# Graph attention layer on one core: P1 is added into bank 6 in PSUM, the results stay in PSUM for elu, and the side tasks of the second projection get another order

## The chip, the cores and the metric

The kernel runs on one core of one Trainium2 chip. The metric is the device time of one execution in microseconds (us), in float32 throughout. Names used below: TensorE (PE, with weight loads listed as PEld), VectorE (DVE), ScalarE (ACT), GpSimd (POOL) and SyncE (SP), which here only issues DMAs. PSUM is the memory that matmuls write; it is used in eight banks of 128 x 512 floats. A matmul can be told to add to what its bank holds.

## The reference

The input x has 128 graphs of 64 nodes with 512 features. It is normalized, attended twice, passed through a feed-forward block and added to itself:

```
h  = relu(layernorm(x))
a1 = 4 heads of graph attention:  Wh = h @ W_heads[k]; e = leaky_relu(f1 + f2); softmax over adjacent nodes; attn @ Wh
h1 = elu(a1), heads side by side (2048 features)
a2 = one head of the same attention with W_out (2048 x 512)
o  = elu(a2)
y  = relu(o @ w1 + b1) @ w2 + b2 + o
x + layernorm(y) * gamma + beta
```

## The kernel before

The 8192 rows are cut into 64 tiles of 128 rows (two graphs each) and 16 groups of four tiles. One group is 512 rows. For each group `g` the loop at the end of the kernel issues two stretches:

- **First projection.** Four heads, each one call of `project1`, with side tasks between. The attention of layer 1 is applied to the inputs ahead of the weights (`attend1` fills the `z` tiles), so a head is one product of 512 x 512 blocks, and its result goes through `elu`. The side tasks are the second attention of the group before (`stage_e`).
- **Second projection.** `project2(g)`: 28 steps, four heads for each of seven products. Beside them run `attend1(g + 1)`, the feed-forward block of group `g - 1` (`feed_forward`, which has the lists `tr` for transposes, `ff` for its 14 products and `fin` for its four `finish` tasks: second layer norm, addition of x, output), and `stage_a(g + 2)`: first layer norm (`norms`), transposes of the normalized rows (`transposes`), scores (`project_f`, `scores1`), two softmaxes of 128 x 512 (`attn_weights`, one for each pair of tiles) and the transposes of the attention weights (`transpose_weights`, called the turn below, one for each pair; TensorE transposes `s1A` into `s1pt`, L469).

Every 512 x 512 product is done by `unit` (L257) with seven products of 256 x 256 blocks instead of eight, after Strassen and Winograd. P1 to P7 go to three PSUM banks, which are named after the product that opens them: bank 1 takes P1 and P2, bank 5 takes P5 and P3, bank 6 takes P6, P7 and P4. The four results are

```
C11 = P1 + P2          C12 = P1 + P6 + P5 + P3
C22 = P1 + P6 + P7 + P5    C21 = P1 + P6 + P7 + P4
```

Before the change ScalarE copies P1 to SBUF (`s1`, L268), VectorE adds it to P5 (`s15`) and to P6 (`t`, both L270), and the results are bank 5 + `t`, bank 6 + `s15` and bank 6 + `s1`, each added by VectorE (L577 in the first projection, L618 in the second, L719 and L733 in the feed-forward block). In the first projection `elu` (L538) follows: two ScalarE instructions (L541, L542) and one of VectorE (L543), which read the sum in SBUF.

The order of the work on each engine comes from two things. The Python code gives each instruction a place in the program, and `run` (L248) deals a list of side tasks out evenly over the steps of a unit. A scheduler then orders the instructions of each engine by priority and by its own estimate of when they are ready; `high_priority(AHEAD)` moves what follows a product ahead by 150 places. The result is one fixed queue for each engine, in which an instruction that waits holds all behind it. Weights come through a ring of 11 slots (L238), issued by SyncE in the order of their use; loads of x (for `norms`) and of `xr` (for `finish`) go through the same SyncE queue and share four slots.

Pools that matter here: PSUM has six banks for units and `attend1`, and two for transposes and scores. The softmax of layer 1 has one buffer for `e` and one for its result `s1A`, so the second softmax of a group can write its result only after TensorE has transposed the first.

Of the kernel before, what the change touches and what calls it, by code (L numbers as in the profile page):

```python
# [22 lines left out]
def gat_preln_kernel(  # L23
# [28 lines left out]
    nc = tc.nc  # L52
# [188 lines left out]

    late = []

    def flush_late():
        while late:
            late.pop(0)()
# [10 lines left out]
    def unit(name, product, post, order):  # L257


        own = {1: 1, 2: 1, 5: 5, 3: 5, 6: 6, 7: 6, 4: 6}  # L260
        gb, sb = {}, {}

        def after(p):
            if p in (1, 5, 6):
                nm = {1: "s1", 5: "s15", 6: "t"}[p]
                sb[nm] = wk.tile([P, 2, T], FP, tag=nm, name=f"{nm}_{name}")
                if p == 1:
                    nc.scalar.copy(sb[nm], gb[1])  # L268
                else:
                    nc.vector.tensor_tensor(sb[nm], gb[p], sb["s1"], ALU.add)  # L270
                post(nm, sb[nm])
            elif p == 2:
                post("c11", gb[1], None)
            elif p == 7:
                post("c22", gb[6], sb["s15"])
            elif p == 3:
                post("c12", gb[5], sb["t"])
            else:
                post("c21", gb[6], sb["s1"])

        def part(p, i, n):
            def fn():
                if i == 0:
                    subs[p] = product(p)
                    if p == own[p]:
                        gb[p] = bank(f"g{p}_{name}")
                subs[p][i](gb[own[p]], p == own[p] and i == 0)
                if i == n - 1:
                    with tc.high_priority(AHEAD):
                        after(p)  # L290
            return fn

        subs = {}
        n = product(None)
        return [part(p, i, n) for p in order for i in range(n)]
# [161 lines left out]
    def attn_weights(p):  # L457
        A1[p] = softmax(E1.pop(p), None, 2 * H, "s1", p)
# [17 lines left out]

    def stage_a(g):

        if g >= NG:
            return []  # L480
        p, r = 2 * g, 2 * g + 1

        def norms(p):
            norm1(2 * p)
            norm1(2 * p + 1)
            if p >= 2:
                prefetch(2 * p + 2)
                prefetch(2 * p + 3)

        def transposes(p):  # L490
            transpose_h(2 * p)
            transpose_h(2 * p + 1)

        wait = [lambda: None]
        return [
            lambda: norms(p), lambda: norms(r), lambda: transposes(p), lambda: transposes(r),
        ] + wait + [lambda: project_f(g)] + wait * 2 + [
            lambda: (scores1(g), attn_weights(p)), lambda: None, lambda: attn_weights(r),
        ] + wait * 2 + [lambda: transpose_weights(p)] + wait * 2 + [lambda: transpose_weights(r)]


    ZB = {}
# [42 lines left out]
    def flat(ap):  # L545
        return ap.rearrange("p a b -> p (a b)")

    def quadrant(what):
        return int(what[1]) - 1, int(what[2]) - 1
# [7 lines left out]
    def project1(g, h):  # L557


        z = ZB[g]  # L560
        first = (g, h) == (0, 0)
        if h == 0:
            for b in ("11", "12", "S1", "22"):
                tag = "hS" if b == "S1" else "h" + b
                H1[b] = big.tile([P, H, 2, T], FP, tag=tag, name=f"h{b}_{g}")
        sums = {6: 0, 7: 1, 3: 2}
        blk = {1: "11", 2: "12", 4: "22", 5: "S1"}

        def post(what, a, b=None):
            if what[0] != "c":  # L570
                return
            nm = {"c11": "11", "c12": "12", "c21": "S1", "c22": "22"}[what]
            dst = H1[nm][:, h]
            if b is None:
                elu(flat(dst), flat(a), f"{what}_{g}_{h}")
            else:
                nc.vector.tensor_tensor(dst, a, b, ALU.add)  # L577
                elu(flat(dst), flat(dst), f"{what}_{g}_{h}")
            if what == "c21":
                nc.gpsimd.tensor_tensor(dst, dst, H1["22"][:, h], ALU.add)  # L580

        s = unit(
            f"a{g}_{h}", product_t(h, lambda p: ZSUM[h][sums[p]] if p in sums else z[blk[p]][:, h]),
            post, (1, 2, 6, 5, 7, 3, 4) if first else (1, 6, 5, 2, 7, 3, 4),
        )

        def next_sums():
            if h + 1 < H:
                z_sums(g, h + 1)

        return [
            s[0], lambda: (s[1](), flush_late()), lambda: (s[2](), next_sums()), s[3], s[4],
            lambda: (s[5](), late.append(s[6])),
        ]
# [4 lines left out]
    def project2(g):  # L599
        slot = {1: "11", 2: "12", 3: "12", 4: "22", 5: "S1", 6: "11", 7: "S1"}  # L600
        h1 = dict(H1)
        wh = big.tile([P, G, FO], FP, tag="wh2", name=f"wh2_{g}")
        WH2[g] = wh

        def post(what, a, b=None):
            behind = {"s1": ("11", "S1", "11"), "s15": ("S1", "22", "11"), "c11": ("12", "12", "11")}
            if what in behind:
                dst, x0, x1 = (h1[n] for n in behind[what])
                for h in range(H):
                    nc.gpsimd.tensor_tensor(dst[:, h], x0[:, h], x1[:, h], ALU.subtract)  # L610
            if what[0] != "c":
                return
            r, c = quadrant(what)
            dst = wh[:, 2 * r:2 * r + 2, c * Q:(c + 1) * Q]
            if b is None:
                nc.scalar.copy(dst, a)
            else:
                nc.vector.tensor_tensor(dst, a, b, ALU.add)  # L618

        ms = [H + h for h in range(H)]  # L620
        return unit(
            f"b{g}", product_n(ms, lambda p, i: h1[slot[p]][:, i]), post, (1, 5, 6, 2, 7, 3, 4)
        )
# [61 lines left out]
    def feed_forward(g):  # L685
# [22 lines left out]

        bl = {}

        def post1(what, a, b=None):
            if what[0] != "c":
                return
            if not RT:
                RT.extend(big.tile([P, KC, T], FP, tag=f"rt{i}", name=f"rt{i}_{g}") for i in range(2))
            r, c = quadrant(what)
            dst = RT[r][:, 2 * c:2 * c + 2]
            if b is not None:
                nc.vector.tensor_tensor(dst, a, b, ALU.add)  # L719
                a = dst  # L720
            for k in range(2):
                nc.scalar.activation(
                    dst[:, k], a[:, k], AF.Relu, bias=b1s[:, 2 * c + k:2 * c + k + 1]
                )
            if what == "c21":
                bl[2] = blocks(RT, f"r{g}")

        def post2(what, a, b=None):

            r, c = {"t": (0, 1), "s15": (1, 1), "s1": (1, 0)}.get(what) or quadrant(what)  # L730
            dst = o[:, 2 * r:2 * r + 2, c * Q:(c + 1) * Q]
            eng = nc.vector if what[0] == "c" else nc.gpsimd
            eng.tensor_tensor(dst, a, dst, ALU.add)  # L733
# [8 lines left out]
            nc.vector.scalar_tensor_tensor(y, y, rstd, xr, ALU.mult, ALU.add)  # L742
            nc.sync.dma_start(out=of[ts(t, P), :], in_=y)

        f1 = unit(f"c{g}", product_t(M1, lambda p: bl[1][p]), post1, (1, 2, 6, 5, 7, 3, 4))
        f2 = unit(f"d{g}", product_n([M2], lambda p, i: bl[2][p]), post2, (1, 6, 5, 2, 3, 7, 4))
        return (
            [lambda j=j: transpose_out(j) for j in range(G)], f1 + f2,
            [lambda j=j: finish(j) for j in range(G)],
# [60 lines left out]
    for g in range(NG):  # L810
        if g >= 1:
            side = stage_e(g - 1)
        else:
            side = stage_a(1)
            for i, m in ((6, 4), (11, 5), (16, 6), (21, 7)):
                side.insert(i, lambda m=m: more_sums(m))
        done, n = 0, 6 * H
        for i in range(n):
# [6 lines left out]
                done += 1  # L825
        flush_late()
        attn = attend1(g + 1) if g + 1 < NG else []
        if g >= 1:
            tr, ff, fin = feed_forward(g - 1)
        else:  # L830
            tr, ff, fin = [], [lambda: more_sums(M1), lambda: None, lambda: more_sums(M2), load_rows], []
        if g < NG - 1:
            early = [lambda: z_sums(g + 1, 0)]
            at = 8 if g >= 1 else 0
            run(project2(g), mix(attn, tr) + mix(ff[:at] + early + ff[at:], stage_a(g + 2)) + fin)
        else:
            run(project2(g), tr + [lambda: None] * 6 + ff[:2])
            run(ff[2:], [
                lambda: [scores2(g, j) for j in range(G)], lambda: spread2(g), lambda: None,
                lambda: None, lambda: softmax2(g),  # L840
                *[lambda: None] * 7, lambda: transpose_weights2(g), lambda: None,
                *[lambda j=j: attend2(g, j) for j in range(G)], lambda: None,
            ])
    last = fin
    tr, ff, fin = feed_forward(NG - 1)
    run(tr + ff[:6] + last + ff[6:12] + fin[:2] + ff[12:] + fin[2:])
# [29 lines left out]
```

## Time and profile before

| | |
|---|---|
| median of 11 runs | 2389.02 us (2383.66 to 2392.91) |
| profiled execution, its own time | 2390.47 us |
| its span in the trace | 2388.7 us, 32881 instructions |
| granted TensorE clock, mean | 0.994 |
| TensorE busy | 97% |
| VectorE busy | 61% |
| GpSimd busy | 44% |
| ScalarE busy | 33% |
| DMA | mean 154 GB/s |

A profile like this is read from the busiest engine outwards. TensorE is almost never idle, so the first question is where its few idle stretches lie and what ends them; the busy shares of the other engines are means over a whole group, and say little about the stretch in which one of them is full. Busy time of matmuls overlaps (each is listed with some 380 ns, and a new one starts every 216 ns), so the starts are what to read in a list of matmuls, not the durations.

### The profile page before, as it was taken

What the parts mean: (1) busy time and instruction counts of PE and PEld (TensorE: products, weight loads), DVE (VectorE), ACT (ScalarE), POOL (GpSimd) and SP (SyncE); (2) the same over time, 40 slices, a digit from 0 to 9 for tenths busy, and PEclk for the clock granted to TensorE, in tenths of its full rate; (3) what the DMA queues carried; (4) which work ended last, traced back from release to release, by engine and by line L of the source; (5) the groups of instructions that cost most, each with busy time, mean ns of one, the idle gap of its engine ahead of it and who ended that gap; (6) DMA issues with size and microseconds to landing.
All of it is one profiled execution on the core that took longest, in us unless ns stands there. A gap on an engine that the chain in (4) does not pass through costs nothing.

```text
span 2388.7 us, 32881 instructions
## 1 busy us (share of the span) xinstructions
PE 2321.7 (97%) x11805; PEld 1941.2 (81%) x11805; DVE 1454.4 (61%) x2418; ACT 780.2 (33%) x1383; POOL 1062.3 (44%) x933
## 2 busy tenths in 40 slices
PE   6989999999999999999999999999999999999997
PEld 4868888888888888888888888888888888888885
DVE  6736475574855747466574855748466574754637
ACT  2423415233151432415233151432415233141412
POOL 5771443435444263443534444264443534533334
PEclk9989999999999999999999999999999999999999
DMA  8554454454544445454454534545454453534442
GB/s 302 184 178 139 133 167 129 141 172 133 172 133 149 160 133 172 129 164 143 139 174 130 176 128 145 169 133 177 130 161 146 137 176 129 176 122 154 163 149 97
DMA packets 257808, 366.89 MB, mean 154 GB/s; under 512 B 22216, under 2 KB 145128, under 8 KB 257648
## 3 DMA queue, kind: packets, MB, share of 16 engines
q1 hardware_dynamic: 251024, 343.82, 44.5%
q0 software_dynamic: 4512, 16.78, 1.9%
q10 hardware_dynamic: 2112, 4.19, 0.5%
q8 instruction: 95, 1.56, 0.3%
q14 instruction: 65, 0.53, 0.1%
HBM read 337.45 MB, written 27.26 MB: 153 GB/s over the span
## 4 chain that ended last, share of the span: by engine, by line
PE 92%; POOL 3%; DVE 2%; issue 1%; DMA 1%; ACT 0%; DVEq 0%; SPq 0%; POOLq 0%; ACTq 0%
PE g_b L319 33%; PE g_a L304 31%; PE g_c L304 8%; PE g_d L319 8%; PE pz L519 4%; PE pa L668 2%; PE pzS L519 1%; PE pto L695 1%; PE pth L368 1%; PE s1pt L469 1%; PE pf L378 1%; DMA pw<-in_L_gnn_w_dram 1%; PE s1pe L403 1%; POOL pt L218 0%; POOL pt L219 0%
## 5 line engine op out<-in xcount | busy, mean ns | idle before, releaser
L319 PE MATMUL g_b<-w,h 128*128 128x256 f32 x2560 | 601.4, 381 | 0.0
L319 PEld LDWEIGHTS g_b<-w,h 128*128 128x128 f32 x2560 | 477.8, 190 | 74.6 <-issue 14.0
L304 PE MATMUL g_a<-zs_z,w 128*128 128x256 f32 x1504 | 352.4, 382 | 18.6 <-issue 16.0
L304 PE MATMUL g_a<-z,w 128*128 128x256 f32 x1520 | 359.5, 379 | 1.0 <-ACT at L471 0.9
L304 PEld LDWEIGHTS g_a<-zs_z,w 128*128 128x128 f32 x1504 | 286.7, 192 | 70.0 <-issue 28.3
L304 PEld LDWEIGHTS g_a<-z,w 128*128 128x128 f32 x1520 | 287.7, 190 | 54.5 <-issue 14.6
L319 PE MATMUL g_b<-w,hS 128*128 128x256 f32 x1024 | 248.0, 389 | 6.4 <-DVE z L531 6.4
L580 POOL TENSOR_TENSOR hS<-hS,h 128x512 f32<-128x512 f32 x64 | 81.6, 1276 | 371.5 <-DVE hS L543 368.3
L319 PEld LDWEIGHTS g_b<-w,hS 128*128 128x128 f32 x1024 | 190.5, 192 | 50.4 <-issue 15.7
L610 POOL TENSOR_TENSOR h<-h,h 128x512 f32<-128x512 f32 x64 | 86.8, 1356 | 227.2 <-PE g_b L319 227.2
L542 ACT ACTIVATE exc<-exc 128x512 f32<-128x512 f32 x256 | 160.6, 627 | 6.0
L543 DVE SCALAR_TENSOR_TENSOR h<-exc,h 128x512 f32<-128x512 f32 x128 | 103.7, 810 | 63.4 <-ACT exc L542 63.3
L541 ACT ACTIVATE exc<-h 128x512 f32<-128x512 f32 x128 | 80.5, 629 | 181.5 <-DVE h L577 181.5
L610 POOL TENSOR_TENSOR h<-hS,h 128x512 f32<-128x512 f32 x64 | 81.6, 1275 | 125.1 <-PE g_b L319 125.0
L330 POOL TENSOR_TENSOR zs_z<-z,zs_z 128x512 f32<-128x512 f32 x63 | 87.3, 1386 | 84.9 <-PE g_d L319 73.7
L329 POOL TENSOR_TENSOR zs_z<-zS,z 128x512 f32<-128x512 f32 x63 | 87.7, 1393 | 81.7 <-PE g_a L304 60.7
L331 POOL TENSOR_TENSOR zs_z<-z,zs_z 128x512 f32<-128x512 f32 x63 | 88.9, 1411 | 78.5 <-PE g_a L304 78.5
L319 PE MATMUL g_d<-w,rt 128*128 128x256 f32 x512 | 121.2, 379 | 1.8 <-DVE o L733 1.0
L304 PE MATMUL g_c<-ot,w 128*128 128x256 f32 x512 | 121.1, 379 | 0.7 <-ACT s_c L268 0.7
L304 PE MATMUL g_a<-zS,w 128*128 128x256 f32 x496 | 117.2, 379 | 0.0
L634 DVE SCALAR_TENSOR_TENSOR jf<-wh,ao 128x512 f32<-128x512 f32 x128 | 111.9, 894 | 0.7
L519 PE MATMUL pz<-at,hn 64*128 64x256 f32 x768 | 108.1, 405 | 3.5 <-DVE z L531 3.5
(163 smaller groups left out, 3660.5 us busy)
## 6 DMA issues: line engine op xcount, KB each, us to landing
w<-tc SPq DMA_DIRECT2D x632, 256.0 KB, 2.7
w<-in_L_gnn_W_heads_dram SPq DMA_DIRECT2D x192, 256.0 KB, 2.9
w<-in_L_gnn_W_out_dram SPq DMA_DIRECT2D x192, 256.0 KB, 2.7
w<-in_L_gnn_w_dram SPq DMA_DIRECT2D x96, 256.0 KB, 2.7
x<-in_x_dram SPq DMA_DIRECT2D x66, 256.0 KB, 2.7
xr<-in_x_dram SPq DMA_DIRECT2D x64, 256.0 KB, 2.8
out_dram<-o SPq DMA_DIRECT2D x64, 256.0 KB, 2.2
tc<-pt POOLq DMA_DIRECT2D x20, 512.0 KB, 4.3
```

The source lines that it names most:

```text
L304: nc.tensor.matmul(bk[:, o, :], w[:, k, ts(o, P)], a[:, k, :], start=start and o == 0 and k == 0, stop=k == 1, skip_group_check=True,)
L319: nc.tensor.matmul(bk[:, j, :], a[:, k, ts(j, P)], w[:, k, :], start=start and k == 0 and j == 0, stop=i == len(ms) - 1 and k == 1, skip_g ...
L329: eng.tensor_tensor(s2, s1, a11, ALU.subtract)
L330: eng.tensor_tensor(s4, a12, s2, ALU.subtract)
L331: eng.tensor_tensor(s3, a22, s2, ALU.subtract)
L519: nc.tensor.matmul(banks[b][:, c, :].rearrange("p (h n) -> p h n", h=H), src[rows, off + c * P:off + (c + 1) * P], at[rows, b], start=True ...
L541: nc.scalar.activation(ex, src, AF.Relu, scale=-1.0)
L542: nc.scalar.activation(ex, ex, AF.Exp, scale=-1.0)
L543: nc.vector.scalar_tensor_tensor(dst, ex, -1.0, src, ALU.add, ALU.max)
L580: nc.gpsimd.tensor_tensor(dst, dst, H1["22"][:, h], ALU.add)
L610: nc.gpsimd.tensor_tensor(dst[:, h], x0[:, h], x1[:, h], ALU.subtract)
L634: nc.vector.scalar_tensor_tensor(junk, WH2[g][:, j], 1.0, ao[:, c, :], ALU.mult, ALU.mult, accum_out=f[:, c, j:j + 1],)
```

## The change

In `unit`, ScalarE still copies P1. VectorE then adds P1 to bank 6 in place, in PSUM, after P6, and ScalarE copies that sum (`t`) and P5 (`s5`) to SBUF. P7 and P4 are accumulated on top, so bank 6 ends as C21 without an addition. C12 is added into bank 5 and C22 into bank 1, and `elu` reads all four results from PSUM. In the second product of the feed-forward block, the addition of `s1` to one quadrant of `o` goes.

The order of the products changes: the first projection and the first feed-forward product go to 1, 5, 6, 2, 3, 7, 4 from 1, 6, 5, 2, 7, 3, 4 and from 1, 2, 6, 5, 7, 3, 4; the second feed-forward product goes to the same from 1, 6, 5, 2, 3, 7, 4. The second projection keeps 1, 5, 6, 2, 7, 3, 4.

`stage_a` returns three lists (norms; transposes and scores; turns), and the side tasks of the second projection are dealt out anew: norms go beside `attend1`; two of the four `finish` tasks go between the last feed-forward products, beside the scores; and the other two `finish` tasks go last, beside the two turns. In group 0, the sums of the feed-forward weights (`more_sums(M1)`, `more_sums(M2)`) go from the beginning of that list to its end, and those of the other weights come a few tasks earlier in the first projection.

```
     def after(p):
         if p in (1, 5, 6):
-            nm = {1: "s1", 5: "s15", 6: "t"}[p]
+            nm = {1: "s1", 5: "s5", 6: "t"}[p]
             sb[nm] = wk.tile([P, 2, T], FP, tag=nm, name=f"{nm}_{name}")
-            if p == 1:
-                nc.scalar.copy(sb[nm], gb[1])
-            else:
-                nc.vector.tensor_tensor(sb[nm], gb[p], sb["s1"], ALU.add)
+            if p == 6:
+                nc.vector.tensor_tensor(gb[6], gb[6], sb["s1"], ALU.add)
+            nc.scalar.copy(sb[nm], gb[p])
             post(nm, sb[nm])
         elif p == 2:
-            post("c11", gb[1], None)
+            post("c11", gb[1])
         elif p == 7:
-            post("c22", gb[6], sb["s15"])
+            post("c22", gb[6], sb["s5"], gb[1])
         elif p == 3:
-            post("c12", gb[5], sb["t"])
+            post("c12", gb[5], sb["t"], gb[5])
         else:
-            post("c21", gb[6], sb["s1"])
+            post("c21", gb[6])
...
 # project1
-            if b is None:
-                elu(flat(dst), flat(a), f"{what}_{g}_{h}")
-            else:
-                nc.vector.tensor_tensor(dst, a, b, ALU.add)
-                elu(flat(dst), flat(dst), f"{what}_{g}_{h}")
+            if b is not None:
+                nc.vector.tensor_tensor(to, a, b, ALU.add)
+                a = to
+            elu(flat(dst), flat(a), f"{what}_{g}_{h}")
...
-            post, (1, 2, 6, 5, 7, 3, 4) if first else (1, 6, 5, 2, 7, 3, 4),
+            post, (1, 2, 6, 5, 7, 3, 4) if first else (1, 5, 6, 2, 3, 7, 4),
...
 # stage_a
+        return (
+            [lambda: norms(p), lambda: norms(r)],
+            [
+                lambda: transposes(p), lambda: transposes(r), nothing, lambda: project_f(g), nothing,
+                lambda: (scores1(g), attn_weights(p)), nothing, lambda: attn_weights(r),
+            ],
+            [nothing, lambda: transpose_weights(p), nothing, nothing, lambda: transpose_weights(r)],
+        )
...
 # side tasks of project2, groups 1 to 14 (before: one line)
-            run(project2(g), mix(attn, tr) + mix(ff[:at] + early + ff[at:], stage_a(g + 2)) + fin)
+        first = mix(attn, tr)
+        first[9:9] = norms[:1]
+        first += norms[1:]
...
+            run(project2(g), first + mix(
+                ff[:7] + early + ff[7:12] + fin[:1] + ff[12:13] + fin[1:2] + ff[13:], scores
+            ) + mix(fin[2:], [nothing] + turns + [nothing] * 2))
...
 # feed_forward
-        f1 = unit(f"c{g}", product_t(M1, lambda p: bl[1][p]), post1, (1, 2, 6, 5, 7, 3, 4))
-        f2 = unit(f"d{g}", product_n([M2], lambda p, i: bl[2][p]), post2, (1, 6, 5, 2, 3, 7, 4))
+        f1 = unit(f"c{g}", product_t(M1, lambda p: bl[1][p]), post1, (1, 5, 6, 2, 3, 7, 4))
+        f2 = unit(f"d{g}", product_n([M2], lambda p, i: bl[2][p]), post2, (1, 5, 6, 2, 3, 7, 4))
```

More of the change, by code (lines that the diff above doesn't have):

```diff
@@ L242, in gat_preln_kernel, with nothing @@
     late = []
+    def nothing():
+        pass
     def flush_late():
@@ L479, in stage_a @@
         if g >= NG:
-            return []
+            return [], [], []
         p, r = 2 * g, 2 * g + 1
@@ L492, in transposes @@
             transpose_h(2 * p + 1)
[L494 to L499, printed above, removed]
+        return (
[6 more added lines that the diff above has]
+        )
     ZB = {}
@@ L567, in project1, with post @@
         blk = {1: "11", 2: "12", 4: "22", 5: "S1"}
-        def post(what, a, b=None):
+        def post(what, a, b=None, to=None):
             if what[0] != "c":
@@ L603, in project2, with post @@
         WH2[g] = wh
-        def post(what, a, b=None):
-            behind = {"s1": ("11", "S1", "11"), "s15": ("S1", "22", "11"), "c11": ("12", "12", "11")}
+        def post(what, a, b=None, to=None):
+            behind = {"s1": ("11", "S1", "11"), "s5": ("S1", "22", "11"), "c11": ("12", "12", "11")}
             if what in behind:
@@ L709, in feed_forward, with post1 @@
         bl = {}
-        def post1(what, a, b=None):
+        def post1(what, a, b=None, to=None):
             if what[0] != "c":
@@ L726, in post1, with post2 @@
                 bl[2] = blocks(RT, f"r{g}")
-        def post2(what, a, b=None):
-            r, c = {"t": (0, 1), "s15": (1, 1), "s1": (1, 0)}.get(what) or quadrant(what)
+        def post2(what, a, b=None, to=None):
+            if what == "s1":
+                return
+            r, c = {"t": (0, 1), "s5": (1, 1)}.get(what) or quadrant(what)
             dst = o[:, 2 * r:2 * r + 2, c * Q:(c + 1) * Q]
@@ L813, in gat_preln_kernel @@
         else:
-            side = stage_a(1)
-            for i, m in ((6, 4), (11, 5), (16, 6), (21, 7)):
+            side = sum(stage_a(1), [])
+            for i, m in ((5, 4), (9, 5), (12, 6), (17, 7)):
                 side.insert(i, lambda m=m: more_sums(m))
@@ L827, in gat_preln_kernel, with sums_late @@
         attn = attend1(g + 1) if g + 1 < NG else []
-        if g >= 1:
-            tr, ff, fin = feed_forward(g - 1)
-        else:
[L831 to L834, printed above, removed]
-            run(project2(g), mix(attn, tr) + mix(ff[:at] + early + ff[at:], stage_a(g + 2)) + fin)
[L836 to L843, printed above, removed]
+        norms, scores, turns = stage_a(g + 2)
+        tr, ff, fin = feed_forward(g - 1) if g >= 1 else ([], [], [])
+        if g == NG - 1:
+            run(project2(g), tr + [nothing] * 6 + ff[:2])
+            run(ff[2:], [
+                lambda: [scores2(g, j) for j in range(G)], lambda: spread2(g), nothing, nothing,
+                lambda: softmax2(g), *[nothing] * 7, lambda: transpose_weights2(g), nothing,
+                *[lambda j=j: attend2(g, j) for j in range(G)], nothing,
+            ])
+            continue
+        early = [lambda: z_sums(g + 1, 0)]
+        first = mix(attn, tr)
+        first[9:9] = norms[:1]
+        first += norms[1:]
+        if g == 0:
+            def sums_late(m):
+                fetch(m)
+                weight_sums(m, LAST["A"])
+            run(project2(g), first + early + scores + turns + [
+                load_rows, lambda: sums_late(M1), lambda: sums_late(M2)
+            ])
+        else:
+            run(project2(g), first + mix(
+                ff[:7] + early + ff[7:12] + fin[:1] + ff[12:13] + fin[1:2] + ff[13:], scores
+            ) + mix(fin[2:], [nothing] + turns + [nothing] * 2))
     last = fin
```

## Prediction, as put on record before the changed kernel ran

> **What bounds the kernel now.** I read the busy shares and the chain first, then the waits of TensorE, then each wait in the order of time on the engine named.
>
> ```profile
> PE 2321.7 (97%) x11805; PEld 1941.2 (81%) x11805; DVE 1454.4 (61%) x2418; ACT 780.2 (33%) x1383; POOL 1062.3 (44%) x933
> PE 92%; POOL 3%; DVE 2%; issue 1%; DMA 1%; ACT 0%; DVEq 0%; SPq 0%; POOLq 0%; ACTq 0%
> ```
>
> TensorE is the bound, and the change leaves it every matmul. So it can win only TensorE's idle time, and lose by adding to it. The waits of TensorE (us in total, times, longest):
>
> ```profile
> PE g_a L304 <- issue: 16.0, 13, 2.2
> PE g_b L319 <- DVE z L531: 6.4, 1, 6.4
> PE pz L519 <- DVE z L531: 3.5, 1, 3.5
> ```
>
> The windows by stage (length, PE busy, PEld, DVE, ACT, POOL, granted clock, DMA share, GB/s) say where the idle time lies:
>
> ```profile
> 0.00:60.00 60.00, 39.74 (x182) 27.80 (x183) 40.78 (x112) 16.98 (x29) 34.78 (x51) 1.00 0.84 302
> 60.00:199.00 139.00, 125.67 (x694) 103.49 (x693) 77.16 (x119) 44.55 (x78) 91.09 (x89) 0.95 0.51 175
> 199.00:2216.00 2017.00, 2001.04 (x10225) 1680.12 (x10224) 1238.27 (x2019) 671.55 (x1191) 873.91 (x744) 1.00 0.46 149
> 2216.00:2389.00 173.00, 155.22 (x709) 129.80 (x708) 98.22 (x171) 47.09 (x85) 62.50 (x50) 0.98 0.41 135
> ```
>
> Idle: 20.3 us in the prologue, 13.3 in group 0, 16.0 in the 2017 us of the steady part, 17.8 in the last group. The 16.0 are the 13 waits put down to "issue", one at each start of a first projection after a feed-forward block (2.1, 1.2, 2.1, 0.9, 2.2, then 0.8 to 1.5). The timeline of VectorE and TensorE at such a place shows what they are:
>
> ```profile
> 1217.79 0.69 DVE L270 TENSOR_TENSOR t_a<-g_a,s_a 128x512 f32<-128x512 f32 x1
> 1218.58 3.69 PE L304 MATMUL g_a<-zs_z,w 128*128 128x256 f32 x16 [0.80 <-issue]
> ```
>
> P7 of head 0 may write bank 6 only after VectorE has read `t` from it, and VectorE is late: it still works on the `finish` tasks. In group 0 it is a DMA and GpSimd that make VectorE late:
>
> ```profile
> 138.46 0.69 DVE L340 BATCH_NORM_STATS2 n1st<-x 128x6 f32<-128x512 f32 x1 [9.72 <-DMA x<-in_x_dram]
> 146.27 0.18 DVE L342 BATCH_NORM_AGGREGATE n1mv<-n1st 128x2 f32<-128x6 f32 x1 [6.53 <-POOL n1nb L354]
> ```
>
> Copies of `z` stand behind both, and TensorE waits for their PSUM banks (6.4 and 3.5 us). Last, the place that the new task order touches, the turns (s1pt) of one group, with the scores that feed them:
>
> ```profile
> 1178.48 1.09 PE L403 MATMUL s1pe<-R,L 64*64 64x256 f32 x16
> 1193.42 1.04 PE L469 MATMUL s1pt<-ident,s1A 128*128 128x128 f32 x8
> 1206.38 1.04 PE L469 MATMUL s1pt<-ident,s1A 128*128 128x128 f32 x8
> ```
>
> ```profile
> 1195.22 0.23 DVE L436 COPY s1A<-s1A 128x128 f32<-128x128 f32 x1
> 1202.61 1.67 DVE L742 SCALAR_TENSOR_TENSOR o<-o,n2rs,xr 128x512 f32<-128x512 f32 x1
> ```
>
> The second softmax ends on VectorE at 1195.45, 10.9 us before its turn at 1206.38: no wait.
>
> [...] the trace has 683 to 691 with one input from PSUM (L270). [...] L742 has a median of 753 ns, a mean of 1192, and up to 1860, with the long one above beside a GpSimd sum. [...]
>
> **The change, part by part.** One product of four matmuls takes 1.73 us on TensorE (starts in the timeline), a turn of two tiles 0.87, the scores 1.0.
>
> *Copies and sums.* There are 112 units (64 + 16 + 16 + 16). The P5 addition goes in all of them, the C21 addition in 96: 208 VectorE instructions of 0.685 us, 142 us. `elu` from PSUM (L543: 682 ns) in place of SBUF (810 and 946) saves 128 x 0.128 + 64 x 0.264 = 33 us. ScalarE gets 224 copies of 0.58 = 130 us. Neither engine is the bound, so this is worth only what TensorE waits for them. An addition that writes PSUM is not in the trace; between 0.6 and 0.8 us, I take 0.69.
>
> *New waits inside a unit.* P7 now needs the addition and then a ScalarE copy, 0.69 + 0.58 and three hand-overs of some 0.15 = 1.7 us. P2 and P3 stand between, 3.46 us. Covered with 1.7 us to spare; in the queues of the changed program I find at most one or two instructions (a softmax exponential, an `elu` of the transposed attention) ahead of the copy. With no cover it would cost 1.7 us x 64. P4 after P7 in the last head of each group has half a product (0.86 us) over C22's addition, which takes 0.2 + 0.69 + 0.1: 0.2 us x 15 = 3 us lost (0 to 5). In the last feed-forward block P4 follows P7 directly (about 1 us lost), and P2 no longer follows P1 (0.7 won): nothing in sum.
>
> *The boundary.* Two `finish` tasks earlier, and two products rather than one between P6 and P7: the 16 us go (13 to 16).
>
> *Group 0.* The feed-forward sums leave this stretch except one fetch, so GpSimd does not stand at a DMA there: 9.9 us (6.4 + 3.5), of which I take 10 (6 to 10). The fetches of W_out keep their places nearly. That the other 2.6 and 0.9 stay is assumed.
>
> *The turns.* In the compiled queue of TensorE the turns of groups 1 to 13 now stand together near the end: after the scores come 10 products, the first turn, one product, the second turn. So the second is due 11 x 1.73 + 0.87 = 19.9 us after the scores (before: 1179.50 to 1206.38, 26.9). In the compiled queue of VectorE, the same in all 13 groups, 42 instructions stand from the first masked addition of the scores (L417) to the last copy of the second softmax (L436): both softmaxes, three additions to `o`, four of each instruction of `finish`, two of L618, one of L634. The last `finish` instruction (L742) stands right before that copy. With the mean of each group, the softmaxes are 2 x (0.681 + 0.864 + 0.686 + 0.781 + 0.686 + 0.202 + 0.843 + 0.256) = 10.0 us. The rest: L733 3 x 0.686, L340 4 x 0.682, L342 4 x 0.163, L344 4 x 0.144, L741 4 x 0.798, L742 4 x 1.192, L618 2 x 0.68, L634 0.97: 16.3. Starts follow each other some 0.06 us closer than these durations: 26.3 - 42 x 0.06 = 23.8. ScalarE's exponential leaves VectorE idle for 0.7 in the first softmax, GpSimd some 0.2 before an L742, the start 0.15: 24.8 us. Three of eight transposes can go before the copy; the other five take 0.54. The turn then ends at 24.8 + 0.1 + 0.54 = 25.4, not at 19.9 + 0.87 = 20.8: TensorE stands 4.7 us in each group. (P4 of the second feed-forward product waits for part of that earlier, behind the same queue; it isn't counted twice.) Behind it everything of the group is late by the same time. Bounds: with no instruction stretched by GpSimd (0.68 to 0.75 in place of the means) the copy ends at 22.0 and the wait is 1.9; with all stretched at 26.5, and 6.3. Loss: 13 x 4.7 = 61 us (25 to 82).
>
> *Sum* against the profiled execution's own 2390.5: + 61 + 3 - 16 - 10 = + 38, 2428.5. The median is 1.5 below that execution: 2427.
>
> **Rivals.** *VectorE keeps up (faster).* Were the 42 instructions done within 20.2 us, the turn would not wait, and 2389 - 26 + 3 = 2366 would be left. For it: VectorE loses 175 of 1454 us. Against it: of these 42, none is removed, and the same kinds took 25 us of busy time between 1180.7 and 1210.8. *It cancels (no change).* With the shortest durations the loss of 25 meets the gain of 26: 2391. *ScalarE becomes late inside the heads.* If the copy of `t` stood behind a late exponential by 2 us in each of 64 heads, 0.3 us each, 20 us more: 2447. Against it: the instructions ahead end earlier by the counting above.
>
> **Numbers.** Likeliest, the late turn: 2427, chance 0.80 with its own range; beyond it, by the second mechanism together with the upper bounds, 0.05; keeping up 0.10; cancelling 0.05. Changes within 0.2%, 4.8 us, are about what can't be told from none. Low end: 13 x 2.6 us lost against 26 won, 2396; high end: 82 + 5 against 22, 2454. Faster 0.10, same 0.05, slower 0.85.
>
> **What would show it.** Right: waits of TensorE at s1pt for VectorE's s1A, some 13 of them, 2 to 6 us each, and none at the start of the first projection; group 0 without the waits for `z`; VectorE busy near 1280 us, ScalarE near 910. Wrong: no waits at s1pt, or idle time at g_a inside the heads, in front of P7, for `t`.

## The result, and the profile after

The changed kernel takes 2411.61 us (median of 8 runs, 2409.27 to 2413.58). The kernel before, measured again beside it, takes 2389.26 us (31 runs). The ratio is 1.0095, with a 95% interval of 1.0086 to 1.0103: slower by about 1%. The profiled execution took 2413.58 us with a span of 2411.8 us, 23.1 us more than the span before. I forecast a loss of 38 us; the sign and the place were right, and most of the sizes were off.

The busy shares of the changed kernel say that TensorE is still the bound, that VectorE lost 249 us of work, and that ScalarE gained 132:

```profile
PE 2340.3 (97%) x11805; PEld 1951.5 (81%) x11805; DVE 1205.2 (50%) x2210; ACT 912.1 (38%) x1623; POOL 1027.7 (43%) x917
```

The waits of TensorE in the changed kernel (us in total, times, longest) say where the time went. The 13 waits at g_a are gone, and there are waits at s1pt for s1A. One of the 14 in the first line, 5.4 us, lies in the prologue, in the kernel before too; the other 13 lie in groups 1 to 13. One wait at a copy of `z` remains in group 0.

```profile
PE s1pt L472 <- DVE s1A L435: 32.5, 14, 5.4
PE pzS L525 <- DVE z L537: 5.7, 1, 5.7
...
PE s1pt L472 <- DVE s1A L439: 1.5, 8, 0.2
```

The timeline of TensorE in one group of the changed kernel (start, duration, engine, line) shows the late turn. From 1063.53 eight matmuls of g_b take 1.73 us, so the second turn was due at 1065.26. It starts at 1067.69, 2.43 us late. Then something appears that I hadn't counted: the sixteen matmuls from 1069.52 take until 1073.65, 4.13 us in place of 16 x 0.216 = 3.46, and no wait is marked.

```profile
1062.66 1.04 PE L472 MATMUL s1pt<-ident,s1A 128*128 128x128 f32 x8
1063.53 1.89 PE L322 MATMUL g_b<-w,h 128*128 128x256 f32 x8
1067.69 2.03 PE L472 MATMUL s1pt<-ident,s1A 128*128 128x128 f32 x8 [2.27 <-DVE s1A L435]
1069.52 4.30 PE L322 MATMUL g_b<-w,h 128*128 128x256 f32 x16
1073.65 1.89 PE L307 MATMUL g_a<-z,w 128*128 128x256 f32 x8
```

The windows of the same stretch (length, then busy time of PE, PEld, DVE, ACT, POOL, then the granted clock, third from the end) show what that is: after the pause the granted clock of TensorE is 0.50 for three microseconds.

```profile
1060.00:1064.00 4.00, 4.00 (x25) 3.56 (x24) 3.05 (x9) 1.16 (x3) 1.96 (x2) 1.00 0.86 259
1064.00:1067.50 3.50, 1.42 (x7) 0.92 (x5) 2.65 (x7) 0.37 (x1) 1.74 (x3) 1.00 0.48 170
1067.50:1070.50 3.00, 2.81 (x11) 2.43 (x12) 3.00 (x10) 1.17 (x2) 0.00 (x0) 0.50 0.68 207
```

VectorE in the same group shows why the copy is late. It ends at 1068.34, 23.05 us after the next product began behind the scores (1045.29); 19.97 us was the time to beat. In that stretch VectorE is full, but for 0.70 us in the first softmax, for ScalarE's exponential, which I had counted, and one wait of 1.80 us for GpSimd's n2rs:

```profile
1062.36 0.69 DVE L623 TENSOR_TENSOR wh<-g_b,t_b 128x512 f32<-128x512 f32 x1
1064.85 0.75 DVE L749 SCALAR_TENSOR_TENSOR o<-o,n2rs,xr 128x512 f32<-128x512 f32 x1 [1.80 <-POOL n2rs L349]
...
1066.86 0.69 DVE L435 TENSOR_TENSOR s1A<-s1e,s1r 128x512 f32<-128x512 f32 x1
...
1068.12 0.22 DVE L439 COPY s1A<-s1A 128x128 f32<-128x128 f32 x1
```

GpSimd's own timeline shows that n2rs stood behind the addition to the next `xr`. SyncE issued that load only at 1058.40, behind the output of an earlier finish task, and the two loads of this stretch took 4.2 to 4.5 us to land, so it came at about 1062.9. The profile names VectorE's last instruction as the releaser here, since the two fall together; of the additions to `xr` that wait, 28 wait for the load.

```profile
1063.05 1.27 POOL L745 TENSOR_TENSOR xr<-xr,bs 128x512 f32<-128x512 f32 x1 [2.04 <-DVE wh L623]
1064.27 0.55 POOL L349 TENSOR_TENSOR n2rs<-n2ve,mhalf 128x1 f32<-128x1 f32 x1
```

By stages, the first projection of group 1 begins 6.8 us earlier than before (192.7 for 199.5), the stretch from there to the last first projection is 33.4 us longer (2044.9 for 2011.5), and the rest is 3.5 us shorter (174.2 for 177.7). The sum is the 23.1 us.

### The profile page after: what moved, and what is told of

It reads as the page before. It is cut to its first block, busy times and chain, and to the rows that moved or that the text cites. A ratio compares the mean times of both kernels' runs of the same rounds, so it can differ in the third digit from the quotient of the medians.

```text
span 2411.8 us, 32882 instructions
## 1 busy us (share of the span) xinstructions
PE 2340.3 (97%) x11805; PEld 1951.5 (81%) x11805; DVE 1205.2 (50%) x2210; ACT 912.1 (38%) x1623; POOL 1027.7 (43%) x917
## 4 chain that ended last, share of the span: by engine, by line
PE 82%; DVE 10%; issue 2%; POOL 2%; DMA 2%; ACT 1%; SPq 0%; DVEq 0%; POOLq 0%
PE g_a L307 31%; PE g_b L322 26%; PE g_c L307 8%; PE g_d L322 5%; PE pz L525 4%; PE pa L673 2%; DVE o L749 2%; DVE o L748 2%; PE pzS L525 1%; DMA xr<-in_x_dram 1%; PE pto L700 1%; PE pth L371 1%; DVE n2st L343 1%; DVE o L740 1%; PE s1pt L472 1%
## 5 line engine op out<-in xcount | busy, mean ns | idle before, releaser
L322 PE MATMUL g_b<-w,h 128*128 128x256 f32 x2560 | 614.7, 387 | 0.0
L322 PEld LDWEIGHTS g_b<-w,h 128*128 128x128 f32 x2560 | 488.1, 194 | 78.1 <-issue 13.0
L547 ACT ACTIVATE exc<-g_a 128x512 f32<-128x512 f32 x256 | 152.3, 595 | 199.4 <-DVE g_a L581 119.1
L549 DVE SCALAR_TENSOR_TENSOR h<-exc,g_a 128x512 f32<-128x512 f32 x192 | 131.6, 685 | 137.7 <-ACT exc L548 136.6
L333 POOL TENSOR_TENSOR zs_z<-z,zs_z 128x512 f32<-128x512 f32 x63 | 88.2, 1401 | 117.0 <-PE g_d L322 74.2
L745 POOL TENSOR_TENSOR xr<-xr,bs 128x512 f32<-128x512 f32 x64 | 84.7, 1324 | 77.5 <-DMA xr<-in_x_dram 68.9
L322 PEld LDWEIGHTS g_d<-w,rt 128*128 128x128 f32 x512 | 96.0, 190 | 17.3 <-DVE o L740 1.4
L428 ACT ACTIVATE s1e<-s1e 128x512 f32<-128x512 f32 x32 | 20.2, 630 | 232.1 <-DVE s1e L427 232.1
```

The costliest lines, as they stand in the source:

```text
L322: nc.tensor.matmul(bk[:, j, :], a[:, k, ts(j, P)], w[:, k, :], start=start and k == 0 and j == 0, stop=i == len(ms) - 1 and k == 1, skip_g ...
L333: eng.tensor_tensor(s4, a12, s2, ALU.subtract)
L547: nc.scalar.activation(ex, src, AF.Relu, scale=-1.0)
L549: nc.vector.scalar_tensor_tensor(dst, ex, -1.0, src, ALU.add, ALU.max)
L745: nc.gpsimd.tensor_tensor(xr, xr, bs, ALU.add)
```

## Experiments

My theory at this point: the second turn is late because of its place behind VectorE's queue. The rivals: the new unit costs the time, or the late `xr` does, or the low clock is an effect of its own. Ratios below are against the kernel before, measured on the same chip in the same series, with 95% intervals. "Period" is the time from one group to the next, read from the starts of the matmul s2pe; with no pause at all it turned out to be 142.26 us.

**The two halves apart.** The first kernel is the changed one with the side tasks, the turns and the sums of group 0 as before; the second is the kernel before with the new side tasks.

```
 # unit_only, against the changed kernel (cut short; stage_a and the sums of group 0 go back too)
-            run(project2(g), first + mix(ff[:7] + early + ... , scores) + mix(fin[2:], ...))
+            run(project2(g), mix(attn, tr) + mix(ff[:at] + early + ff[at:], stage_a(g + 2)) + fin)
 # order_only, against the kernel before: the same lines, exchanged
```

> The change of the unit alone (P1 added in PSUM, the new copies, the new orders of products), with the side tasks of the second projection and the sums of group 0 dealt out as in the kernel before. Late turn (my theory): 19 VectorE instructions stand between the scores and the second turn, and the turn is due some 27 us after the scores, so no wait at the turns; the 13 waits at the start of the first projection shrink (P7 comes one product later, the copy costs 0.9 us more), from 16 to 5 us or less; group 0 keeps its waits for copies of z. About 2378 us, 2370 to 2386, faster than the kernel before. Rival, the unit costs it (longer chains, more of ScalarE, other order of products): 2400 us or more.

> The order of the side tasks alone (and the moved sums of group 0), with the unit and the orders of products of the kernel before. Late turn: the same 42 VectorE instructions stand between the scores and the second turn, due 19.9 us after the scores, and more of them are slowed beside GpSimd than in the changed kernel, since VectorE has the additions from SBUF: a wait of 3.4 to 5 us in each of 13 groups, +44 to +65, less some 7 in group 0 and up to 16 at the start of the first projection: 2410 to 2432 us. Rival, the unit costs it: the order of the tasks gains, 2366 to 2385 us.

Measured: the unit alone 2379.74 us, ratio 0.9984 (0.9978 to 0.9991); the order alone 2411.84 us, ratio 1.0111 (1.0096 to 1.0126). The two add up to the whole, -0.16% and +1.11%. The unit is no cost, and the order is all of it. Two things were unexpected. The unit alone keeps the waits at the first projection, only at another product: P4 of the first head now waits for VectorE's addition of C22, which reads the bank that P4 adds to.

```profile
PE g_a L307 <- DVE g_a L578: 13.5, 12, 1.3
PE g_b L322 <- DVE z L534: 10.7, 1, 10.7
```

And the order alone shows the low clock at its plainest, on TensorE: a pause of 1.54 and 0.19 us, and then sixteen matmuls in 5.06 us (1066.83 to 1071.89) that need 3.46.

```profile
1065.44 0.52 PE L472 MATMUL s1pt<-ident,s1A 128*128 128x128 f32 x3 [1.54 <-DVE s1A L435]
1066.15 0.89 PE L472 MATMUL s1pt<-ident,s1A 128*128 128x128 f32 x5 [0.19 <-DVE s1A L439]
1066.83 5.22 PE L322 MATMUL g_b<-w,h 128*128 128x256 f32 x16
```

**The turns early.**

```
-                ff[:7] + early + ff[7:12] + fin[:1] + ff[12:13] + fin[1:2] + ff[13:], scores
-            ) + mix(fin[2:], [nothing] + turns + [nothing] * 2))
+                ff[:7] + early + ff[7:12] + fin[:1] + ff[12:13] + fin[1:2] + ff[13:], scores + turns
+            ) + fin[2:])
```

> The changed kernel with the two turns dealt out with the scores beside the products of the feed-forward block, and the last two finish tasks after them: 22 VectorE instructions in place of 42 before the second turn, which is due some 30 us after the scores. Late turn: the 13 waits of 3.4 us go, 2411.6 - 44 = 2367 us (2363 to 2376), faster than both kernels. Rival, the unit costs it: the same as the changed kernel, 2405 to 2415. Rival, the two finish tasks now last delay the t of the first head: waits at the start of the first projection of 1 to 2 us come back, 2380 to 2393.

Measured: 2354.8 us, ratio 0.9877 (0.9863 to 0.9890), below the range of the expectation: 57 us under the changed kernel where 44 was expected (52 by the two ratios, since the kernel before took 2383.79 us in this series and 2389.26 beside the changed kernel). Each group loses 4.5 us less, not 3.4, since the low clock goes with the pause. Some 0.4 us a group goes that no wait accounts for. The starts of TensorE's matmuls have it where one shape of matmul follows another: the small products of `attend1` (pz) stand in six stretches of each group here, and in seven in the changed kernel. In the steady part TensorE does not stop at all, as the window shows (busy time is the whole length):

```profile
199.00:2180.00 1981.00, 1981.00 (x10172) 1669.44 (x10171) 1031.75 (x1826) 780.94 (x1395) 843.28 (x734) 1.00 0.46 152
```

**The same queue, one product later.** VectorE's 42 instructions stay as they are.

```
-            ) + mix(fin[2:], [nothing] + turns + [nothing] * 2))
+            ) + mix(fin[2:], [nothing] * 2 + turns + [nothing]))
```

> The changed kernel with both lists as they are, but the second turn one product of TensorE (1.73 us) later; the queue of VectorE keeps its 42 instructions between the scores and the last copy. In the changed kernel TensorE stands some 2.4 us for the first copy of s1A and 0.4 for the last, and its granted clock is then at 0.50 for some 3 us, another 1.2 to 1.7 us lost: 4.5 us in a group. Queue against due time, with the clock: the pause falls to 0.6 to 1.1 us, too short for the clock to fall, 1.0 to 1.6 us lost in a group: 2411.6 - 13 x 3.2 = 2370 us (2366 to 2376). Pause alone, the clock costs nothing: only the 1.73 us of each group are saved, 2389 us (2386 to 2394).

Measured: 2373.48 us, ratio 0.9950 (0.9936 to 0.9963). One product of 1.73 us saves 3.0 us a group (period 143.8 for 146.8), and the low clock is gone. This fits the clock theory (2366 to 2376) and not the pause alone (2386 to 2394). TensorE's timeline has the short pauses, and 0.216 us a matmul behind them (1055.88 to 1057.60 for eight):

```profile
1054.57 0.52 PE L472 MATMUL s1pt<-ident,s1A 128*128 128x128 f32 x3 [0.58 <-DVE s1A L435]
1055.27 0.77 PE L472 MATMUL s1pt<-ident,s1A 128*128 128x128 f32 x5 [0.19 <-DVE s1A L439]
1055.88 1.89 PE L322 MATMUL g_b<-w,h 128*128 128x256 f32 x8
1057.60 1.89 PE L307 MATMUL g_a<-z,w 128*128 128x256 f32 x8
```

**The late xr.**

```
 # finish(j)
-            xr = load(t, "xr")
+            if j == 0:
+                for k in range(G):
+                    XR[t + k] = load(t + k, "xr")
+            xr = XR.pop(t)
 # norms(p): two of the four loads of x, for the next group, go behind the finish tasks
```

> The changed kernel with the four loads of xr in a group issued together at the first finish task, and two loads of x moved behind the finish tasks to make room; places of turns and finish tasks kept, and the second turn still due 11 products after the scores. It takes away the 1.8 us that VectorE stands in the 42 instructions for GpSimd's n2rs, which stands behind an addition to a late xr; 38 instructions then stand before the copy. If the queue and that wait make the turn late: the wait of 3.4 us per group falls to 0 to 1.6, 2367 to 2390 us. If the wait for GpSimd is not part of it (VectorE would have been late anyhow): 2405 to 2412.

Measured: 2371.26 us, ratio 0.9947 (0.9933 to 0.9960), period 143.5. In twelve groups the turn is late by 0.6 us only, and the clock stays up. In the last, VectorE has 40 instructions rather than 38 before the copy and waits for GpSimd again, and the turn is 2.8 us late. The wait for GpSimd, 1.8 us in a queue that was 2.6 us too late, may thus have decided whether the late turn was dear; but the queue is shorter by four instructions too, and this run does not separate the two.

Both repairs in one:

> Both repairs in one: turns early, and the four loads of xr together at the first finish task (its loads of x moved behind the finish tasks). If the late xr cost time only through the late turn, there is nothing left for it to win, since TensorE has no pause left in groups 1 to 13: 2352 to 2357 us, the same as with the turns early alone. If late xr costs something of its own: 2340 to 2350. If the x loads, now later, delay the norms: 2360 or more.

Measured: 2365.85 us, ratio 0.9916 (0.9902 to 0.9929). This is 11 us worse than the turns early alone. The later loads of x make VectorE wait inside the norms (2.62 us in one group), C22's addition stands behind that, and in three groups TensorE stands 1.5 us at P4 of the first head for it. The rest is 0.44 us in each group (period 142.7 for 142.26), with no wait in the list: the list is dealt out differently, pz stands in seven stretches again, and the 0.44 us lie in the starts where the shape of matmul changes, 41 times in a group for 39. A load moved out of the way of one queue came late in another.

**All four finish tasks last.** This asks what removed the waits at the first projection.

```
-                ff[:7] + early + ff[7:12] + fin[:1] + ff[12:13] + fin[1:2] + ff[13:], scores + turns
-            ) + fin[2:])
+                ff[:7] + early + ff[7:], scores + turns
+            ) + fin)
```

> The kernel with the turns early, but all four finish tasks behind the feed-forward products, as in the kernel before. If the 13 waits at the start of the first projection came from VectorE's four finish tasks, they are back, now at P4 of the first head (1.1 to 1.4 us each, as with the unit alone): 2354.8 + 13 x 1.3 = 2372 us (2368 to 2378). Rival, the new unit and its order of products removed them: 2353 to 2358 us.

Measured: 2409.86 us, ratio 1.0104 (1.0084 to 1.0124). The waits are back, so the earlier place of two finish tasks is needed to remove them. They are far dearer than I expected: 34.7 us in 13 waits at P7, and the low clock behind them. VectorE shows why. The statistics of the next x stand 5.78 us for their load, which SyncE issues at 1071.79, behind the outputs of the late finish tasks (1069.14), and the addition of P1 stands next in the queue; ScalarE's copy of it and TensorE's P7 follow at once:

```profile
1077.31 0.69 DVE L343 BATCH_NORM_STATS2 n1st<-x 128x6 f32<-128x512 f32 x1 [5.78 <-DMA x<-in_x_dram]
1077.92 0.68 DVE L272 TENSOR_TENSOR g_a<-g_a,s_a 128x512 f32<-128x512 f32 x1
...
1079.33 3.78 PE L307 MATMUL g_a<-zs_z,w 128*128 128x256 f32 x8 [3.46 <-ACT t_a L273]
```

**Group 0.** Three runs, all on the kernel with the turns early. First the sums at their old places:

```
-            for i, m in ((5, 4), (9, 5), (12, 6), (17, 7)):
+            for i, m in ((6, 4), (11, 5), (16, 6), (21, 7)):
...
-            run(project2(g), first + early + scores + turns + [load_rows, lambda: sums_late(M1), lambda: sums_late(M2)])
+            run(project2(g), first + mix(early + [lambda: more_sums(M1), nothing, lambda: more_sums(M2), load_rows], scores + turns))
```

> The kernel with the turns dealt out early (2354.8 us), but the weight sums of group 0 at their places of the kernel before. Sums in group 0: TensorE's waits for copies of z return (6.4 and 3.5 us in the kernel before, 5.7 with the sums moved), 5 to 9 us lost, all of it before the first projection of group 1: 2360 to 2364 us. Rival, the 7 us won ahead of group 1 came from the task order or the unit and not from the sums: 2353 to 2357 us.

Measured: 2354.54 us, ratio 0.9871 (0.9857 to 0.9885), the same as with the sums moved. In place of one wait of 5.7 us at pzS there are two, 3.3 at pzS and 2.4 at g_a. In this kernel, then, moving the sums wins nothing. Next, loads of x on ScalarE's queue:

```
-        nc.sync.dma_start(out=tl, in_=xf[ts(t, P), :])
+        queue = nc.scalar if name == "x" and 2 * G <= t < 3 * G else nc.sync
+        queue.dma_start(out=tl, in_=xf[ts(t, P), :])
```

> The kernel with the turns early (2354.8 us), but the four loads of x for group 2 are issued by ScalarE's queue and not by SyncE's. In every kernel so far SyncE issues the first of them only at 130.5 us, behind eight loads of transformed weights, and copies of z on VectorE stand behind its statistics. If that queue is the cause of TensorE's 5.7 us at pzS in group 0: the wait goes, with the low clock after it up to 8 us won, 2346 to 2351 us. Rival, as my prediction put it, GpSimd's sums make VectorE late there: 2353 to 2357 us, the same.

Measured: 2355.89 us, ratio 0.9893 (0.9879 to 0.9908), nothing won: these were the wrong loads, and SyncE still issued the one in question, at 132.2 us. The scheduler takes norms up a group ahead. The loads of the next group are the right ones (`3 * G <= t < 4 * G`):

> As the run before with loads of x on ScalarE's queue, but now those of group 3: the compiled queue of VectorE shows that the statistics that stand among the copies of z in group 0 are those of tile 12, taken up a group ahead. Its slot is free when the first layer norm of tile 8 ends (124.8 us), SyncE issues its load at 130.7, 5.9 us later, behind loads of transformed weights. If SyncE's queue is the cause of the 5.7 us at pzS: the load lands some 6 us earlier, the wait falls to 0 to 1, with the low clock after it 5 to 8 us won against 2354.8: 2347 to 2350 us. Rival, GpSimd or the transfer is late: 2353 to 2357 us.

Measured: 2348.76 us, ratio 0.9850 (0.9836 to 0.9863). Two timelines show it. With the turns early, SyncE issues the load at 130.66 and VectorE waits 12.06 us; here ScalarE's queue issues it at 124.77, and VectorE waits 5.35. (In the kernel before, SyncE issued the load behind the 9.72 us of the prediction at 130.89, after five loads of transformed weights.)

```profile
130.66 0.41 SPq L95 DMA_DIRECT2D x<-in_x_dram  x1
136.30 0.69 DVE L343 BATCH_NORM_STATS2 n1st<-x 128x6 f32<-128x512 f32 x1 [12.06 <-DMA x<-in_x_dram]
```

```profile
124.77 0.35 ACTq L96 DMA_DIRECT2D x<-in_x_dram  x1
129.53 0.69 DVE L344 BATCH_NORM_STATS2 n1st<-x 128x6 f32<-128x512 f32 x1 [5.35 <-DMA x<-in_x_dram]
```

TensorE's 5.7 us at pzS shrink to one wait of 2.0, and all that follows is 6 us earlier. This version is the fastest of all, 1.5% below the kernel before.

## Why the prediction was right or wrong

- **The late turn: right in mechanism, mis-sized by errors that partly cancel.** Turn due 19.9 us after the scores: measured 19.97. Queue of 42 instructions: the same. "24.8 us" to the end of the copy was too long: 23.05 in the group shown. In the mean of the 13 groups the 42 instructions take 23.4 us and not 26.3. The largest part of that is 1.8 us: I had taken L742 at its mean of 1192 ns, and the same instruction, now L749, has a mean of 766 in the changed kernel (in the kernel before 33 of the 64 stood beside a GpSimd instruction of over 0.9 us for more than half of their time, with a mean of 1610 ns, and 25 met none, 745; in the changed kernel 15, 834, and 48, 746). Another 1.0 is the softmaxes, which I had taken at means too. Against that I had allowed 0.9 us for VectorE's waits, and 2.3 came, 1.8 of them before an L749 in the group shown, where I had 0.2. So the pause was mis-sized: 4.7 predicted, 2.6 measured (gaps between starts, less the matmuls in them: 2.25 before the first transpose and 0.38 before the fourth, the mean of the 13 groups). The term that was missing is the low clock, 1.5 us on average in 12 of the 13 groups (what is left of the gaps, 18 us). Together 52 us for the predicted 61. "The second turn is late" is shown by the run with one product more, which keeps the queue and changes the due time.
- **The boundary: right that the waits go, wrong in the second of its reasons.** I gave two finish tasks earlier, "and two products rather than one between P6 and P7". The unit alone has the new order and keeps 13.5 us of waits; most of them only move from P7 to P4. All four finish tasks last brings them back. So the place of the finish tasks did it. The way differs, though. In the kernel before, VectorE has no wait for a load in the 9 us ahead of any of the 13 waits: there it is its queue alone, as I wrote. In the unit alone it stands 2.6 to 3.6 us for a late x ahead of each of the 12, and with all four last 3.8 to 6.1 ahead of the twelve longest. The gain was more than 16 as well: behind two of the three longest waits of the kernel before, the clock was low too, 1.7 us each, some 19 in all.
- **Middle part.** 52 less 19 is 33, and 33.4 were measured.
- **"P4 after P7 in the last head", 3 us: none.** No such wait is listed, and the group without pauses has none of it. (The sum was off as well: 0.99 less 0.86 is 0.13 us, 2 us in 15 groups.)
- **Group 0: 10 predicted, 6.8 measured, and the cause was wrong.** The sums at their old places cost nothing, in the kernel with the turns early. The wait that stayed, 5.7 us, comes in the main from a load of x that stood in SyncE's queue behind transformed weights, which the last run shows; a wait of 2.0 us is left without it. How the new order of tasks won its part of 6.8 us stays open: by the starts of s2pe, group 1 is 6.4 us earlier with the order alone, and 2.8 with the unit alone.
- **Tail: 0 predicted, 3.5 us won.** The unit wins it: from the s2pe of group 13 on, the unit alone takes 296.0 us, the changed kernel 295.8, the kernel before 299.3. TensorE's waits say where: 2.4 us at g_c for VectorE's `t_c` and 0.8 at g_d, both in the feed-forward block of the last group, are there in the kernel before and in the order alone, and in no kernel with the new unit. I had put this block at nothing: 1 us lost, 0.7 won.
- **Unit: right.** The addition that writes PSUM takes 694 to 700 ns (0.69 taken), ScalarE's copies 581 to 586 (0.58), ScalarE is busy for 912 us (910), and no wait of TensorE for `t` is listed. VectorE lost 249 us, not 175; of the difference L749 alone is 27 (64 x 0.426). The hand-overs, estimated at some 0.15 us each, are 0.09 and 0.06 with all four finish tasks last: the late addition ends at 1078.60, the copy runs from 1078.69 to 1079.27, and P7 starts at 1079.33. P7 and P4 do add onto the sum that VectorE wrote to PSUM: C21 is read from bank 6 with no addition behind them, and VectorE has 208 instructions fewer in all (2210 for 2418).

The difference of 15 us to the forecast is thus 9 from the turn, 3 from the boundary, 3 from P4, 3.5 from the tail, less 3 from group 0.

## What to carry to other kernels

When a task is moved, count what stands between its input and its result in the queue of each engine, and compare that with the time until it is due on the engine that sets the end; a large queue is harmless until the due time passes it, and then each microsecond counts. Before putting the consumer last, look in the queue in front of it for an instruction that waits for a load issued late: here it was a statistic or an addition to `xr`. What helped was to move the consumer, its due time or (with a somewhat shorter queue) the load; taking 249 us of work off VectorE did not prevent the late turn. Price a pause of TensorE of about 2 us with the slow matmuls behind it, not by its length alone (here 1.5 us behind 2.6).

## What the runs showed of the hardware

The low clock after a short pause was not expected. Pauses of 1.6 to 2.9 us (the first gap at the turn, or at P7 in the kernel before) were followed by a granted clock of 0.50 for 3.4 us in 12 of 13 groups of the changed kernel, 9 of 13 of the order alone and 2 of 4 in the kernel before. One group of the changed kernel shows it by its absence: a pause of 1.99 us at full clock, and a period of 145.1 us, where the others have 146.5 to 147.3. Pauses of 1.5 us and less, as in the unit alone (0.91 to 1.43), were not followed by it in any group.

The first gap alone does not settle it. In groups 1 to 13 of the kernel before and of the changed kernel the clock falls 14 times, and in the 3.41 us up to each fall TensorE had stood for 2.1 to 2.9 us in all, by the starts of its matmuls, short gaps included. These windows are of the turn of the changed kernel shown above (length, PE busy, and the clock third from the end):

```profile
1064.06:1067.48 3.42, 1.36 (x7) 0.86 (x5) 2.63 (x7) 0.31 (x1) 1.68 (x3) 1.00 0.48 169
1067.48:1070.89 3.41, 3.20 (x12) 2.73 (x13) 3.38 (x11) 1.17 (x2) 0.00 (x0) 0.50 0.63 193
```

In the last turn with the xr early, though, TensorE stands for 2.77 us in one piece, from 2052.62 to 2055.39, and the clock stays up: the sixteen matmuls from 2056.76 take until 2060.22, 0.216 us each.

```profile
2049.17 3.62 PE L322 MATMUL g_b<-w,h 128*128 128x256 f32 x16
2055.39 0.52 PE L472 MATMUL s1pt<-ident,s1A 128*128 128x128 f32 x3 [2.61 <-DVE n2ve L347]
2056.16 0.77 PE L472 MATMUL s1pt<-ident,s1A 128*128 128x128 f32 x5 [0.25 <-DVE s1A L439]
2056.76 3.62 PE L322 MATMUL g_b<-w,h 128*128 128x256 f32 x16
2060.22 1.89 PE L307 MATMUL g_a<-z,w 128*128 128x256 f32 x8
```

What decides between the two is not shown. No run moved a pause on purpose, and the prologue, where TensorE has other work and long waits, is left out.

VectorE beside GpSimd shows in the kernel before, again by the GpSimd instructions of over 0.9 us. The 45 of L543 that write `hS` with both inputs in SBUF and met none took 692 ns in the mean, and the 19 that stood beside one for more than half of their time 1545. With one input in PSUM (`h<-exc,g_a`) it was 685 in 40 and 675 in 21.
